# Layer 3's first values made in layer 2's last unit, in other tiles, and its position bias in tiles of two heads

## The chip, the cores and the metric

The kernel runs on one NeuronCore of a Trainium2 chip. The metric is the device time of one execution in microseconds (us). Five engines run side by side, each with its own queue of instructions: TensorE (PE, matrix products), VectorE (DVE), ScalarE (ACT), GpSimd (POOL) and SyncE (SP, which here only issues DMAs). Data lie in SBUF (128 partitions), and matrix products are written to PSUM, which this kernel uses as eight banks of 128 partitions by 512 numbers of float32.

## The reference

The input x has shape [8, 512, 128]. Four layers follow one another, each x = x + s * silu(ffn), where s is a token mixer and both are computed from the normalised x. Layers 0 and 1 are attentions with mixtures of experts. Layer 2 is a gated delta rule (a recurrence over chunks of the sequence) with a mixture of eight experts. Layer 3 is:

```python
def _L3_attn_ref(x, Wq, Wk, Wv, Wo, bo, rel_pos_bias):   # x: [8, 512, 128], 16 heads of 64
    q = (x @ Wq).reshape(B, T, H, dh).transpose(0, 2, 1, 3)
    k, v = ...                                             # the same with Wk, Wv
    logits = jnp.einsum('bhqd,bhkd->bhqk', q, k)
    logits = (logits + causal + bias) / dh                 # bias depends on i - j, clipped at 128
    probs = jax.nn.softmax(logits, axis=-1)
    out = jnp.einsum('bhqk,bhkd->bhqd', probs, v).transpose(0, 2, 1, 3).reshape(B, T, H * dh)
    return out @ Wo + bo

def _L3_ffn_ref(x, w_gate, w_up, w_down):                  # hidden size 384, weights dequantised
    return jnp.einsum('bsh,dh->bsd', silu(gate) * up, wd)
```

## The kernel before

**The order of the work.** PE's instructions run in the order in which the program writes them (`manual_schedule`); DVE, ACT, POOL and SP are put in order by a scheduler that works from its own estimates. Pieces of work are Python generators: `step(g, n)` issues the next n pieces of g, `drain(g)` all that are left. So where a piece is stepped decides where its matmuls stand in PE's queue.

**Tiles.** A pool hands out buffers by tag: a tag with one buffer (`bufs=1`, the default of pool `wf`) can be given to a second tile only when the first one's last reader is done, and what writes the second tile waits for that. Pool `wk` is opened and closed with each layer, so that layer 3's `wk` and `lp` tiles lie in memory that layer 2's pools give up at their end; pool `wf` ("wk23") lives through layers 2 and 3. `psS` is a pool of six PSUM banks with one tag, `psA` of two. `evac` (L73) copies a bank to SBUF, by turns with ACT (L77) and DVE (L79).

**Layer 2** has eight units u (half of the batches, a quarter of the sequence). In unit u's twelve half-rounds, `rounds` (L1074) steps by turns the scan (`delta_scan`, L1644: per chunk pk, rhs, pu, U, pn, stn, po), the experts, the inverse of unit u+1, the front of unit u+2, the output of unit u−1 (`delta_output`, L1684) and the combination of the experts (`combine2`, L1405: POOL gathers rows of the experts' results through indirect DMAs, L1341, two tiles g per unit of two buffers each, so the gathers of unit u wait for the reads of unit u−2; DVE L1434 to L1438 and ACT L1436 weigh them; POOL adds to x, L1441). In the last unit, u = 7, one piece of `weights3` (L1958) is stepped in each half-round: layer 3's weights are loaded into `wf` tiles that layer 2 no longer needs, those of the feed-forward net are dequantised and transposed (L1986), and batch 0 is normalised (`normed3`, L1781: DVE L109 to L118, then four transposes ptxnT and one copy to xnT). What is left of the generators is drained after unit 7, `weights3` last: the output of unit 7 (Vb scaled by POOL L1699, poT, pg, s), the combination, and the rest of `weights3`.

Of the tiles of layer 2 that matter here, `chan0` (the keys and queries by channel, [P, 2, 512] in all), `Kd` ([P, 512]) and `AO` ([P, 512]) lie in `wk` with three buffers each, `chan1` and the rest in `wf`.

**Layer 3** (`layer3`, L1731) first has the bias loaded: `position_bias` makes one tile of 16 heads x 512 per partition in `lp`, of which DVE clears the first 256 columns (four memsets, L1954) and SP loads the others (four DMAs). Then `inputs3(0)` (L1788) makes the values of batch 0: eight products pv of 128x512, for the four row tiles t and the two halves i of the heads (i = 0: heads 0 to 7), each copied by `evac` into a tile v3 of `wk`. After that comes one loop over half steps r; new, i = divmod(r, 2) is a group (b, g) of two heads of batch b and half i of its rows:

- `scores3` of the group: PE writes ps (one bank for i = 0, four for i = 1), DVE adds the bias and finds the greatest (L1833), ACT takes the exponentials (L1837), POOL scales by the sum (L1840).
- `summed3`, four half steps behind: av, the products of the probabilities and v. Group g uses heads 2g and 2g + 1, so groups 0 to 3 use v of i = 0 and groups 4 to 7 of i = 1.
- `transposed3`, three half steps behind: transposes ptp (L1850) in two banks or three, each copied to PT by `evac`.
- for i = 0, `project3` of the next group: pq and pk, each copied by `evac`; and, in every other group, a piece of `ffn3`: pg and pu, read by ACT L1904 and DVE L1905 and L1906.
- for i = 1, `projected3` of an earlier group, and two pieces of `inputs3(b + 1)`, which starts with group 0 of batch b and so has made the next batch's pv by b's group 5 or so.

All of ps, ptp, pq, pk, pg, pu, po, pv and ptxnT take their banks from `psS`; av and the sum of projections have one bank each in `psA`.

Of the kernel before, what the change touches and what calls it, by code (L numbers as in the profile page):

```python
# [9 lines left out]
F32 = mybir.dt.float32  # L10
I32 = mybir.dt.int32
AF = mybir.ActivationFunctionType
ALU = mybir.AluOpType
AX = mybir.AxisListType

B, S, D = 8, 512, 128
# [15 lines left out]
def tile_kernel(ctx: ExitStack, tc: tile.TileContext, w: dict, out: bass.AP):  # L32
# [1021 lines left out]
    def layer2():  # L1054
        nonlocal wk, fw, sm2
        with ExitStack() as lx:
            lp = lx.enter_context(tc.tile_pool(name="l2", bufs=1))
            fw = lx.enter_context(tc.tile_pool(name="fw2", bufs=3))
            wk = lx.enter_context(tc.tile_pool(name="wk2", bufs=1))
            sm2 = lx.enter_context(tc.tile_pool(name="sm2", bufs=4))  # L1060
            dram = lx.enter_context(tc.tile_pool(name="dram2", bufs=1, space=bass.MemoryType.DRAM))
            c = dict(lp=lp, dram=dram, units={}, xn_d=shared["xn_d"], rs2=shared["rs2"], lg=shared["lg"], ln=shared["ln"])
            c["eo_d"] = dram.tile([8 * CAP + 1, D], F32, name="l2eo_d")
            c["idx_d"] = dram.tile([P, CAP // 16], F32, name="l2idx_d")
            c["s_d"] = dram.tile([2 * NT, P, 4 * D], F32, name="l2s_d")
            with tc.manual_schedule(engines={mybir.EngineType.PE}):
                front = delta_front(0, c)
                step(front)
                loaded2(c)
                N = 2 * NT  # L1070
                out = iter(())
                weights = weights3()

                def rounds(u, experts, combined, n_experts):  # L1074
                    nonlocal out
                    scan = delta_scan(u, c)
                    inverse = delta_inverse(u + 1, c) if u + 1 < N else iter(())
                    front = delta_front(u + 2, c) if u + 2 < N else iter(())
                    for r in range(12):
                        step(scan)  # L1080
                        step(experts)
                        if not u and r > 1:
                            step(experts)
                        step(inverse)
                        if r > 1:
                            step(front)
                        if r % 3 < n_experts:
                            step(experts)
                        step(out)
                        if u > 3:  # L1090
                            step(combined)
                        if u == N - 1:
                            step(weights)
                    drain(scan, inverse, front, out)
                    out = delta_output(u, c)

                with tc.tile_pool(name="route2", bufs=1) as rp:
                    routed = route2(rp, c)
                    drain(front)
                    front = delta_front(1, c)  # L1100
                    for _ in delta_inverse(0, c):
                        step(front)
                    drain(front)
                    rounds(0, routed, iter(()), 0)
                    drain(routed)
                with tc.tile_pool(name="ex2", bufs=1) as ep:
                    experts = experts2(ep, c)
                    combined = combine2(ep, c)
                    for u in range(1, N):
                        rounds(u, experts, combined, 1)  # L1110
                    drain(out, experts, combined, weights)
# [338 lines left out]
    def delta_front(u, c):  # L1450
# [71 lines left out]
        for i, parts in enumerate((((0, None, G), (1, gam, V)), ((0, beta, G), (1, None, V)))):  # L1522
            byt = wf.tile([P, 2, 4, 4, 32], F32, tag="byt", name=f"byt{i}{nm}", bufs=1)
            for k, part in enumerate(parts):
                scaled(byt[:, k], *part)
            x = (wf if i else wk).tile([P, 2, 4, 4, 32], F32, tag=f"chan{i}", name=f"chan{i}{nm}", bufs=1 if i else 3)
            V.transpose(x.rearrange("p a c h i -> p (a c h i)"), byt.rearrange("p a c h k -> p (a c h k)"))
            chan.append(x)
        r["KT"], r["QgT"] = chan[0][:, 0], chan[0][:, 1]
        kd = r["Kd"] = wk.tile([P, 4, 4, 32], F32, tag="Kd", name=f"Kd{nm}", bufs=3)  # L1530
        scaled(kd, 0, wend, G)
        Vb = r["Vb"] = wk.tile([P, 4, 4, 64], F32, tag="Vb", name=f"Vb{nm}", bufs=4)
        G.tensor_tensor(Vb, y[:, :, 256:].rearrange("p c (h k) -> p c h k", k=64), bcast(hbeta.rearrange("p (c h) -> p c h", h=4), 3, 64), ALU.mult)
# [2 lines left out]
    def delta_inverse(u, c):  # L1536
# [21 lines left out]
        def level():  # L1558
            n = len(ao)
            if n < 5:  # L1560
                a = wk.tile([P, 16, 32], F32, tag="AO", name=f"AO{nm}_{n}", bufs=3)
                G.tensor_tensor(a, AT, bcast(c["lv"][:, n, :], 1, 16), ALU.mult)
                ao.append(a)

# [166 lines left out]
    def layer3():  # L1731
        nonlocal wk
        with ExitStack() as lx:
            lp = lx.enter_context(tc.tile_pool(name="l3", bufs=1))
            wk = lx.enter_context(tc.tile_pool(name="wk3", bufs=2))
            c = dict(lp=lp, v={}, qk={}, P={}, PT={}, th={}, s={}, **shared["w3"])
            c["bias"] = position_bias(lp, shared["bias"])
            bo = lp.tile([1, NT, D], F32, name="l3bo")
            for t in range(NT):
# [7 lines left out]
            n = 2 * len(groups)  # L1747

            with tc.manual_schedule(engines={mybir.EngineType.PE}):
                drain(inputs3(0, c))  # L1750
                for k in "qk":
                    project3(k, *groups[0], c)
                ffn, done, inputs = iter(()), iter(()), iter(())
                for r in range(n + 7):
                    new, i = divmod(r, 2)
                    if new < len(groups):
                        b, g = groups[new]
                        if g == 0 and i == 0:
                            inputs = inputs3(b + 1, c) if b + 1 < B else iter(())
                            ffn = ffn3(b, c)  # L1760
                        scores3(b, g, i, c)
                    for lag, stage in ((4, summed3), (3, transposed3)):
                        if 0 <= r - lag < n:
                            stage(*groups[(r - lag) // 2], (r - lag) % 2, c)
                    if i == 0:
                        for k in "qk" if new + 1 < len(groups) else "":
                            project3(k, *groups[new + 1], c)
                        if g % 2 == 0:
                            step(ffn)
                    at = r - 7  # L1770
                    if at >= 0 and i:
                        projected3(*groups[at // 2], c)
                        if groups[at // 2][1] == 7:
                            done = finish3(groups[at // 2][0], c)
                    if i:
                        step(inputs, 2)
                    else:
                        step(done)
                drain(ffn, done)
# [7 lines left out]

    def inputs3(b, c):  # L1788

        if b:  # L1790
            yield from normed3(b, c)
        v = c["v"][b] = wk.tile([P, NT, 1024], F32, tag="v3", name=f"v3_{b}")
        for t in range(NT):
            for i in range(2):
                pv = psS.tile([P, S], F32, tag="S", name=f"pv3_{b}_{t}_{i}")
                mm(pv, c["xnT"][b][:, t * P : (t + 1) * P], c["wv"][:, i * S : (i + 1) * S])
                evac(v[:, t, i * S : (i + 1) * S], pv)
                yield

    def project3(n, b, g, c):  # L1800
# [6 lines left out]
    def scores3(b, g, i, c):  # L1807
# [22 lines left out]
        parts = [(2 * n + j, c["P"][b, g, j][:, qb * N[qb] // 2 : qb * N[qb] // 2 + N[qb]], pss[j, qb], j, qb)  # L1830
                 for n, qb in enumerate(qbs) for j in range(2)]
        for n, p, src, j, qb in parts:
            V.tensor_tensor_reduce(p, src, c["bias"][:, 2 * g + j, (3 - qb) * P :], 1.0, NEG, ALU.add, ALU.max, mx[:, n : n + 1])  # L1833
            if n % 2:
                V.tensor_scalar(mx[:, n - 1 : n + 1], mx[:, n - 1 : n + 1], -1.0, None, ALU.mult)  # L1835
        for n, p, _, _, _ in parts:
# [31 lines left out]
    def summed3(b, g, i, c):  # L1868
# [3 lines left out]
        for kb in ((0,), (1, 3, 2))[i]:  # L1872
            k, at = PLACES[kb]
            for j in range(2):
                h = 2 * g + j
                mm(c["av"][64 * j : 64 * j + 64, kb * P :], c["v"][b][:, kb, 64 * h : 64 * h + 64],
                   c["PT"][b, g, j, k][:, at : at + S - kb * P], start=kb == 0, stop=kb == 2)
        if i:
            x = c["aT", b, g] = wk.tile([P, S], F32, tag="aT", name=f"aT3_{b}_{g}")
# [67 lines left out]
    def position_bias(pool, flat):  # L1947


        n = 3 * P  # L1950
        bias = pool.tile([P, H8, S], F32, name="l3bias")
        skewed = flat[:, 0 : P * (n - 1)].rearrange("h (p n) -> p h n", n=n - 1)
        for h in range(0, H8, 4):
            V.memset(bias[:, h : h + 4, 0 : 2 * P], 0.0)  # L1954
            nc.sync.dma_start(bias[:, h : h + 4, 2 * P :], skewed[:, h : h + 4, P - 1 : 3 * P - 1])
        return bias

    def weights3():  # L1958
# [21 lines left out]
        for raw, (n, key, _, tag) in zip(raws, names):  # L1980
# [6 lines left out]
            c[key] = wf.tile([P, NT, P], F32, tag=tag, name=f"l3{n}")[:, 0:3, :]  # L1987
            evac(c[key], pt[:, 0 : 3 * P].rearrange("p (c o) -> p c o", o=P))
            yield
        c["xnT"] = {}  # L1990
        yield from normed3(0, c)

    with tc.tile_pool(name="x12", bufs=1) as x12:
        with tc.tile_pool(name="fw", bufs=8) as fw:
# [27 lines left out]
```

## Time and profile before

| what | us |
| --- | --- |
| median of 3 runs | 3906.91 (3903.22 to 3912.37) |
| the profiled execution | 3900.36 |
| its span | 3898.6 |
| PE busy | 3563.5 (91%), 32622 matmuls |
| DVE, ACT, POOL busy | 2321.6, 1780.3, 1457.5 |
| granted clock of PE over the span | 0.952 |

The profile is one execution, taken by the hardware profiler. A timeline row reads: start, duration (of all that are merged in the row), engine, line, operation, written tile <- read tiles, shapes, count, and in brackets how long the engine was idle before it and what ended that. Times of a row count from the start of the span. A row of stretches gives its bounds, its length, busy time of PE, PEld (weight loads), DVE, ACT and POOL, the granted clock of PE as a share of its full speed, the DMA engines' busy share and GB/s. On the page's PE and PEclk rows each digit stands for a fortieth of the span, in tenths. Layer 2's scan of unit 7 ends near 3054, layer 3's first scores begin at 3095.32, and its steady part lasts to about 3889.

### The profile page before, as it was taken

What the parts mean: (1) busy time and instruction counts of PE and PEld (TensorE: products, weight loads), DVE (VectorE), ACT (ScalarE), POOL (GpSimd) and SP (SyncE); (2) the same over time, 40 slices, a digit from 0 to 9 for tenths busy, and PEclk for the clock granted to TensorE, in tenths of its full rate; (3) what the DMA queues carried; (4) which work ended last, traced back from release to release, by engine and by line L of the source; (5) the groups of instructions that cost most, each with busy time, mean ns of one, the idle gap of its engine ahead of it and who ended that gap; (6) DMA issues with size and microseconds to landing.
All of it is one profiled execution on the core that took longest, in us unless ns stands there. A gap on an engine that the chain in (4) does not pass through costs nothing.

```text
span 3898.6 us, 84883 instructions
## 1 busy us (share of the span) xinstructions
PE 3563.5 (91%) x32622; PEld 1701.0 (44%) x32622; DVE 2321.6 (60%) x7395; ACT 1780.3 (46%) x3916; POOL 1457.5 (37%) x2072
## 2 busy tenths in 40 slices
PE   5999999999999999999999986589886699999998
PEld 2444344444344333333333333456665455555555
DVE  5556656665656555556555664554555766666665
ACT  1355454455454545455555553122221355555554
POOL 1234334334443423333333333453464533333333
PEclk7999999999999999999999997799997899999999
DMA  4100101100011232322222222012112200000000
GB/s 114 46 10 31 31 11 30 30 19 26 27 40 49 78 94 76 84 74 70 69 72 72 71 76 68 5 30 52 32 41 63 48 1 4 4 4 4 4 4 6
DMA packets 139059, 162.93 MB, mean 42 GB/s; under 512 B 29835, under 2 KB 79666, under 8 KB 138528
## 3 DMA queue, kind: packets, MB, share of 16 engines
q1 hardware_dynamic: 135328, 150.69, 13.5%
q0 software_dynamic: 3328, 6.82, 1.0%
q8 instruction: 258, 4.23, 0.5%
q14 instruction: 145, 1.19, 0.1%
HBM read 129.84 MB, written 29.96 MB: 41 GB/s over the span
## 4 chain that ended last, share of the span: by engine, by line
PE 74%; DVE 13%; POOL 5%; issue 3%; ACT 3%; SPq 1%; DMA 1%; POOLq 0%; DVEq 0%; ACTq 0%
PE pt L82 12%; PE ph L82 12%; PE po L82 10%; PE av L82 10%; PE ps L82 8%; PE ptp L1850 3%; PE py L82 3%; PE pk L82 2%; PE s L82 2%; PE pq L82 2%; ACT P L1837 2%; PE pv L82 2%; DVE P L1833 1%; PE pY L82 1%; PE pth L552 1%
## 5 line engine op out<-in xcount | busy, mean ns | idle before, releaser
L522 DVE CUSTOM_DVE_ANT_0 l0junk<-ps,l0junk 128x512 f32<-128x512 f32 (+3 forms) x1024 | 502.1, 490 | 383.2 <-PE ps L82 311.9
L1012 POOL TENSOR_TENSOR h<-h,C 128x512 f32<-128x512 f32 x256 | 326.0, 1273 | 641.4 <-ACT h L1010 592.4
L578 ACT ACTIVATE PT<-pt 128x512 f32<-128x512 f32 (+1 forms) x768 | 360.7, 524 | 405.9 <-PE ps L82 365.4
L829 DVE TENSOR_REDUCE nm<-ps 128x1 f32<-128x512 f32 x512 | 331.6, 684 | 268.2 <-PE ps L82 267.3
L1840 POOL TENSOR_SCALAR P<-P,l 128x128 f32<-128x128 f32 (+3 forms) x512 | 262.7, 532 | 516.6 <-DVE l L1838 360.6
L82 PE MATMUL ps<-l0kA,l0qA 32*128 32x128 f32 (+3 forms) x2048 | 417.7, 486 | 16.7 <-DVE mx L522 11.3
L1837 ACT ACTIVATE P<-P,mx 128x128 f32<-128x128 f32 (+3 forms) x512 | 281.3, 550 | 300.3 <-DVE mx L1835 294.7
L582 POOL TENSOR_SCALAR_AFFINE_SELECT PT<-PT 128x256 f32<-128x256 f32 x512 | 202.0, 407 | 496.1 <-ACT PT L578 494.2
L82 PE MATMUL pt<-l0qA,l0kA 32*128 32x512 f32 (+3 forms) x2048 | 374.4, 470 | 2.1 <-DVE nm L829 1.2
L82 PE MATMUL ps<-l1kA,l1qA 32*128 32x512 f32 x1024 | 333.9, 651 | 33.0 <-DVE nm L829 31.9
L867 ACT ACTIVATE PT<-pt 128x512 f32<-128x512 f32 x512 | 275.9, 595 | 159.5 <-PE ps L82 130.2
L82 PE MATMUL av<-PT,vl0v 128*9 128x512 f32 (+3 forms) x3072 | 315.3, 498 | 1.2 <-POOL PT L582 1.2
L82 PE MATMUL ph<-xnT,l1e 128*128 128x512 f32 x512 | 292.3, 654 | 7.9 <-DVE H L856 3.2
L82 PE MATMUL pt<-l1qA,l1kA 32*128 32x512 f32 x1024 | 272.3, 645 | 0.3 <-ACT PT L867 0.3
L1010 ACT ACTIVATE h<-h 128x512 f32<-128x512 f32 x272 | 171.3, 630 | 217.1 <-DVE h L1007 194.0
L82 PE MATMUL po<-h,l1e 128*128 128x512 f32 x512 | 266.0, 601 | 0.0
L82 PEld LDWEIGHTS pt<-l0qA,l0kA 32*128 32x128 f32 x2048 | 165.6, 185 | 207.2 <-DVE mx L522 66.9
L1833 DVE CUSTOM_DVE_ANT_0 P<-ps,l3bias 128x128 f32<-128x128 f32 (+3 forms) x512 | 225.2, 486 | 39.5 <-PE ps L82 37.5
L671 POOL TENSOR_TENSOR h<-h,C 128x512 f32<-128x512 f32 x128 | 163.1, 1275 | 81.9 <-ACT h L669 63.5
L82 PEld LDWEIGHTS ps<-l0kA,l0qA 32*128 32x128 f32 x2048 | 164.7, 190 | 55.3 <-DVE mx L522 37.0
L669 ACT ACTIVATE h<-ph,l0b 128x512 f32<-128x512 f32 x192 | 131.9, 687 | 100.8 <-PE ph L82 98.4
L82 PE MATMUL av<-PT,v 128*64 128x128 f32 (+3 forms) x1024 | 173.1, 445 | 4.4 <-ACT PT L77 2.6
(523 smaller groups left out, 6368.6 us busy)
## 6 DMA issues: line engine op xcount, KB each, us to landing
C<-wd SPq DMA_DIRECT2D x288, 256.0 KB
qd<-qf SPq DMA_DIRECT2D x24, 256.0 KB
kd<-kf SPq DMA_DIRECT2D x24, 256.0 KB
l0qA<-qd SPq DMA_DIRECT2D x256, 16.0 KB
l0kA<-kd SPq DMA_DIRECT2D x256, 16.0 KB
l2e<-in_L_ffn_w_dram SPq DMA_DIRECT2D x16, 256.0 KB
l3flat<-l3short SPq DMA_DIRECT2D x16, 192.0 KB
l2eo_d<-eo SPq DMA_DIRECT2D x8, 320.0 KB
```

Of the source, the lines that this page charges most:

```text
L82: T.matmul(out_, lhsT, rhs, start=start, stop=stop)
L522: V.tensor_tensor_reduce(c["junk"][:, : (qb + 1) * P], pss[j][:, at], c["mask"][:, (3 - qb) * P :], 1.0, NEG, ALU.add, ALU.max, mx[i][:, q ...
L578: A.activation(p[:, j % 2, :N], pss[j][:, :N], AF.Exp)
L582: G.affine_select(out=own, in_=own, compare_op=ALU.is_ge, fill=0.0, base=0, pattern=[[0, 2], [1, P]], channel_multiplier=-1)
L671: G.tensor_tensor(h, h, C[b, e], ALU.mult)
L829: V.tensor_reduce(nm[g][:, j, qb : qb + 1], pss[j], AX.X, ALU.max, negate=True)
L867: A.activation(Pt[j // 2][:, j % 2, :], pss[j], AF.Exp)
L1010: A.activation(h, h, AF.Square)
L1012: G.tensor_tensor(h, h, C[b, u - u % 2][:, u % 2, :], ALU.mult)
L1833: V.tensor_tensor_reduce(p, src, c["bias"][:, 2 * g + j, (3 - qb) * P :], 1.0, NEG, ALU.add, ALU.max, mx[:, n : n + 1])
L1837: A.activation(p, p, AF.Exp, bias=mx[:, n : n + 1], accum_out=l[:, n : n + 1])
L1840: G.tensor_scalar(p, p, l[:, n : n + 1], 1.0, ALU.mult, ALU.mult)
```

## The change

Three things:

1. In unit 7 two pieces of `weights3` are stepped per half-round instead of one, and `weights3` ends with `inputs3(0)`, not just `normed3(0)`: the eight pv of batch 0 are issued there, and `layer3` no longer does it.
2. `chan0`, `Kd` and `AO` move to `wf`; `chan0` and `Kd` get three tags of one buffer instead of one tag of three. The values of even batches are put into tiles with the tags chan00 and chan02 (asked for once per i, [P, 2, 512] each, of which the half i is used), Kd0, Kd2, and two of AO's buffers; the values of odd batches into a single tile v3 (`bufs=1`; it had two buffers).
3. The bias lies in eight tiles of two heads, l3bias0 in the tag chan01 of `wf` and the seven others in `lp`, with eight memsets and eight DMAs.

```diff
@@ rounds (layer 2)
                         if u == N - 1:
-                            step(weights)
+                            step(weights, 2)
@@ delta_front, delta_inverse
-            x = (wf if i else wk).tile([P, 2, 4, 4, 32], F32, tag=f"chan{i}", name=f"chan{i}{nm}", bufs=1 if i else 3)
+            x = wf.tile([P, 2, 4, 4, 32], F32, tag="chan1" if i else f"chan0{u % 3}", name=f"chan{i}{nm}")
...
-        kd = r["Kd"] = wk.tile([P, 4, 4, 32], F32, tag="Kd", name=f"Kd{nm}", bufs=3)
+        kd = r["Kd"] = wf.tile([P, 4, 4, 32], F32, tag=f"Kd{u % 3}", name=f"Kd{nm}")
...
-                a = wk.tile([P, 16, 32], F32, tag="AO", name=f"AO{nm}_{n}", bufs=3)
+                a = wf.tile([P, 16, 32], F32, tag="AO", name=f"AO{nm}_{n}", bufs=3)
@@ layer3
-                drain(inputs3(0, c))
                 for k in "qk":
                     project3(k, *groups[0], c)
@@ inputs3
-        if b:
-            yield from normed3(b, c)
-        v = c["v"][b] = wk.tile([P, NT, 1024], F32, tag="v3", name=f"v3_{b}")
+        yield from normed3(b, c)
+
+        if b % 2:
+            v = wk.tile([P, NT, 2, S], F32, tag="v3", name=f"v3_{b}", bufs=1)
+            v = [v[:, t, i, :] for t in range(NT) for i in range(2)]
+        else:
+            v = [wf.tile([P, 2, S], F32, tag=f"chan0{u}", name=f"v3_{b}_c{u}")[:, i, :] for u in (0, 2) for i in range(2)] + [wf.tile([P, S], F32, tag=f"Kd{u}", name=f"v3_{b}_k{u}") for u in (0, 2)] + [wf.tile([P, S], F32, tag="AO", name=f"v3_{b}_a{i}", bufs=3) for i in range(2)]
+        c["v"][b] = v
         for t in range(NT):
             for i in range(2):
...
-                evac(v[:, t, i * S : (i + 1) * S], pv)
+                evac(v[2 * t + i], pv)
@@ position_bias
-        bias = pool.tile([P, H8, S], F32, name="l3bias")
+        bias = [pool.tile([P, 2, S], F32, name=f"l3bias{g}") if g else wf.tile([P, 2, S], F32, tag="chan01", name="l3bias0")
+                for g in range(H8 // 2)]
...
-        for h in range(0, H8, 4):
-            V.memset(bias[:, h : h + 4, 0 : 2 * P], 0.0)
-            nc.sync.dma_start(bias[:, h : h + 4, 2 * P :], skewed[:, h : h + 4, P - 1 : 3 * P - 1])
+        for g, x in enumerate(bias):
+            V.memset(x[:, :, 0 : 2 * P], 0.0)
+            nc.sync.dma_start(x[:, :, 2 * P :], skewed[:, 2 * g : 2 * g + 2, P - 1 : 3 * P - 1])
@@ weights3
-        c["xnT"] = {}
-        yield from normed3(0, c)
+        c["xnT"], c["v"] = {}, {}
+        yield from inputs3(0, c)
```

The indexing of v and of the bias in `summed3` and `scores3` follows the new tiles; the products and their order are the same.

More of the change, by code (lines that the diff above doesn't have):

```diff
@@ L1735, in layer3 @@
             wk = lx.enter_context(tc.tile_pool(name="wk3", bufs=2))
-            c = dict(lp=lp, v={}, qk={}, P={}, PT={}, th={}, s={}, **shared["w3"])
+            c = dict(lp=lp, qk={}, P={}, PT={}, th={}, s={}, **shared["w3"])
             c["bias"] = position_bias(lp, shared["bias"])
@@ L1832, in scores3 @@
         for n, p, src, j, qb in parts:
-            V.tensor_tensor_reduce(p, src, c["bias"][:, 2 * g + j, (3 - qb) * P :], 1.0, NEG, ALU.add, ALU.max, mx[:, n : n + 1])
+            V.tensor_tensor_reduce(p, src, c["bias"][g][:, j, (3 - qb) * P :], 1.0, NEG, ALU.add, ALU.max, mx[:, n : n + 1])
             if n % 2:
@@ L1875, in summed3 @@
                 h = 2 * g + j
-                mm(c["av"][64 * j : 64 * j + 64, kb * P :], c["v"][b][:, kb, 64 * h : 64 * h + 64],
+                mm(c["av"][64 * j : 64 * j + 64, kb * P :], c["v"][b][2 * kb + h // 8][:, 64 * (h % 8) : 64 * (h % 8) + 64],
                    c["PT"][b, g, j, k][:, at : at + S - kb * P], start=kb == 0, stop=kb == 2)
```

## The prediction

> **What bounds the kernel now.** I read four views. First the page: its share of busy time by slice, and its chain.
>
> ```profile
> PE   5999999999999999999999986589886699999998
> PEclk7999999999999999999999997799997899999999
> ```
>
> ```profile
> PE 74%; DVE 13%; POOL 5%; issue 3%; ACT 3%; SPq 1%; DMA 1%; POOLq 0%; DVEq 0%; ACTq 0%
> ```
>
> PE carries the end nearly everywhere. It falls off only in the stretch of slices 24 to 32, layer 2 (a slice is 97.5 us); the change touches that layer's last unit and the hand-over to layer 3 (3028 to 3096, slice 32). Then the stretches: columns are busy time of PE, PEld, DVE, ACT and POOL, granted clock, DMA share, GB/s.
>
> ```profile
> 3054.00:3069.20 15.20, 0.08 (x2) 0.01 (x1) 9.28 (x57) 1.52 (x3) 12.50 (x15) 0.57 0.51 65
> 3096.50:3889.00 792.50, 783.89 (x4416) 436.21 (x4416) 519.95 (x1829) 452.77 (x1350) 272.65 (x520) 1.00 0.01 3
> ```
>
> In layer 3 PE is busy 783.89 of 792.50 us: any new wait of PE there is paid in full, once for each of the 64 groups (a batch's two heads) that it touches. Third, PE's and POOL's timelines over the hand-over:
>
> ```profile
> 3055.94 0.94 POOL L1341 DMA_INDIRECT g<-l2eo_d,l2row  x1 [0.30 <-issue]
> ...
> 3067.23 1.91 POOL L1699 TENSOR_TENSOR Vb<-Vb,on 128x1024 f32<-128x1024 f32 x1
> ```
>
> ```profile
> 3069.19 1.12 PE L1713 MATMUL poT<-ident,Vb 128*128 128x128 f32 x4 [15.12 <-POOL Vb L1699]
> ...
> 3088.09 3.78 PE L82 MATMUL pv<-l3wvq,xnT 128*128 128x512 f32 x4 [5.46 <-ACT v L77]
> ...
> 3095.32 1.14 PE L82 MATMUL ps<-kT,qT 64*128 64x128 f32 x8 [0.72 <-ACT kT L77]
> ```
>
> PE idles 15.12 us until POOL has issued the last gathers of the experts' rows and scaled Vb. Then layer 2's last output, its combine (DVE, then POOL's x, ending at 3087.42), and only then layer 3's first copy of v, since its tiles lie in memory that layer 2 gives up last. Last, a group of layer 3 (batch 2, group 4), PE and ACT:
>
> ```profile
> 3336.42 1.14 PE L82 MATMUL ps<-kT,qT 64*128 64x128 f32 x8
> 3337.49 1.08 PE L82 MATMUL av<-PT,v 128*64 128x512 f32 x4
> 3338.50 1.53 PE L1850 MATMUL ptp<-ident,P 128*128 128x128 f32 x12
> 3339.86 1.02 PE L82 MATMUL pq<-xnT,l3wvq 128*128 128x512 f32 x2
> 3340.73 1.02 PE L82 MATMUL pk<-xnT,l3wk 128*128 128x512 f32 x2
> ```
>
> ```profile
> 3339.23 0.40 ACT L1837 ACTIVATE P<-P,mx 128x128 f32<-128x128 f32 x1 [2.98 <-DVE mx L1835]
> ...
> 3341.21 1.04 ACT L77 COPY PT<-ptp 128x512 f32<-128x512 f32 x2
> ```
>
> PE never waits here, though ACT empties ptp only after the four exponentials: six PSUM banks (pool psS) let PE write pk before that copy.
>
> **Part 1: eight pv into unit 7.** Removed after layer 2's end: 16 pv matmuls and their copies. Before, they filled 3077.22 to 3091.66, but beside the combine, so the path loses only what lies behind POOL's last x at 3087.42: the v copies of ACT (1.56) and PE's last four (3.78). DVE's four l3bias memsets end at 3091.83 (1.07 apart) and stand ahead of DVE's v copies and of qT (3094.08). In the changed order seven memsets of 512 elements stand there. Bounds for one: 0.53 (half of 1.07) and 1.07; I take 0.62, as half the work and the 0.16 gap stay. That is 4.3 in place of 4.3, and the copies of 2.42 go; but fourteen small operations of batch 1's normalisation (0.11 each, as pairs of 0.22 to 0.24) move ahead of the first scores. Gain here 0.8 (2.42 less 14 times 0.11, and less 0.06 of memsets).
>
> Added in unit 7: in PE's written order ptxnT and the pv now stand among the scan's matmuls, and whatever they wait for holds back the scan behind them. ptxnT needs the four gl of DVE (2.70 us in this trace, ending 3049.15, between POOL's x and gathers); the scan's pu behind it ran at 3045.74, and goes to about 3049.6. The first pv wait for the copy of ptxnT, the matmuls take 0.9 each at the full clock and up to 1.8 at half, and four v copies on DVE (0.69 each, after the 0.66 of DVE's copies in layer 3) stand ahead of the g operation of L1437, which ends at 3054.82 and which POOL's gathers at 3055.94 wait for, because it frees their tile. Walking this chain: pu's 3.9 and two pv behind it (0.9 to 1.0 each) put the last chunk's pk from 3049.54 to about 3055.3; from there to L1437's end it is 5.3 as before (3049.54 to 3054.82, DVE full, the v copies in the place of PE's waits), so 3060.6 to 3060.7. The gathers begin near 3060.9 instead of 3055.94: +5.0 for them, Vb, poT and the combine behind. A gl that leaves the combine's chain gives back 0.4, projections q and k between the output's matmuls cost 0.5. Sum: +5.0 + 0.5 − 0.4 − 0.8 = **+4.3**. Bounds: −1 if POOL's slack of 1.1 (3054.82 to 3055.94) and idle PE take it all; +9 if the pv run at the half clock (eight more times 0.5 to 0.9).
>
> **Part 2: where v lies.** Even batches ask for the tiles chan00 and chan02 of [P,2,S] twice each, once for each i, and use one half. Each tag has one buffer. So the second (i = 1, heads 8 to 15) cannot be written until every av of the first (heads 0 to 7, groups 0 to 3) has run. In the built order ACT's copy of pv_0_0_1 indeed stands among the exponentials of group 5, likewise for batches 2, 4, 6. Until then two pv sit in PSUM: **two of psS's six banks are held** (a pv of 512 columns fills one), for batch 0 from unit 7 to group 4, for batches 2, 4, 6 from group 2 or 3 of the batch before to group 4: 34 of 64 groups run on four banks.
>
> What that costs I get by giving each layer 3 tile the bank that the built kernel gives it, with its start and its release from this trace, and delaying PE where the bank is still full. The group above as a sample: pk must now wait for the first PT copy. Two take 1.04 from 3341.21, the second starting 0.46 to 0.58 after the first; the first ends at 3341.78, so pk starts 1.05 late (plus 0.06, the usual pause between a copy's end and PE). Then the last ps (3344.57) waits for h L1906, at 3344.75: 0.18 to 0.24. The group pays 1.35. Over the layer: batches 2 and 4 pay 5.4 and 5.7, batch 6 4.3, batches 1, 3, 5 1.2 each (their later half), batch 0 5.1 from group 2 on: 24.2 with the pause, 21.5 without. I take **+21.5**. Bounds: 14, if the delayed PE lets ACT and DVE catch up (ACT is 57% busy, DVE 65%), 26 with the pause and its repeats. Groups 0 and 1 of batch 0, where the pipeline fills: **+2.5** (0 to 3.5).
>
> **Part 3: the clock.** PE pauses of 1.1 to 1.7 us (1.2 to 2.5 in a group) now come in about ten groups, and smaller ones in a dozen more. Rows of this trace: between 3011.85 and 3025.50 the clock was 0.50, though PE was busy 8.32 of 13.65 us and no pause among these matmuls was above 2.33. In all stretches of 3.41 us at the full clock, the next was at half in 30 of 31 where PE was busy under half, 10 of 19 between 0.5 and 0.6, 4 of 14 to 0.7, 2 of 35 to 0.8. A pause of 1.1 leaves 0.68, one of 1.7 leaves 0.5. Some five drops, each 1.7 to 2.5 us (half of what PE does in such a stretch at half clock): **+5**, from 0 to 18 (one drop in each of the eight to ten heaviest groups).
>
> The Trainium skill, "TensorE: Matmul & The Clock Gate", section "Why this matters for your kernels", asks only for no idle gap above about 3 us. By it this term would be nothing and the sum 28; the stretch at 3011.85 speaks against it.
>
> **Part 4: the bias in tiles of two heads.** Eight DMAs for four; seven go at layer 2's release as the four did, and the first group needs only heads 0 and 1, loaded early. L1833's instructions keep number, size and order. Nothing, covered by ps 8 us behind the release; if the cover went, a DMA's delay of some 2 us (sr<-l2s_d, 2.58 on the chain), inside the range.
>
> **Sum:** 4.3 + 21.5 + 2.5 + 5 = +33.3 on the profiled 3900.36 (span 3898.6): 3933.7. That run lies 6.55 under the median of the three shown (3906.91; 3903.22 to 3912.37), so 3940.
>
> **Rivals.**
> (a) *Four banks are enough*: the copies keep ahead, PE's wait shrinks to nothing, and only the hand-over counts: 3906.91 + 4.3 = 3911, or 3906 with −1, not slower by a measurable amount. For it: ACT and DVE are idle over a third of the layer. Against: the idle time lies before the exponentials (2.98), not after. It decides where PT's first copy ends before pk's start: it would have to come 1.05 earlier.
> (b) *The change does what it says*, v is out of PSUM at once, and L1437 isn't delayed. The 7.87 between layer 2's release (3087.45) and the first ps (3095.32) shed 0.8 if the memsets stay as in part 1, up to 7 if nothing of layer 3's start is behind them: 3900 to 3906. Against: the double request of one buffer, and ACT's built order.
> (c) *The clock drops in most groups that pause*: 18 in place of 5, 3953.
> (d) *Unit 7's pv run at half clock* and gathers start 9 later: 3945.
>
> **How the numbers follow.** My forecast (3926 to 3948) 0.58; (c) 0.15; (d) 0.12; a smaller bank cost, 14 or less with no clock drop (3915 to 3926), 0.07; (a) 0.05; (b) 0.03. Leaving out (a), (b) and the far end of (c): 3916 to 3957. A measurement of this kernel tells 0.2%, 7.8 us, from no change. Faster beyond it: (b) with a little more than I worked out, 0.02. Within it (to 3914.7): (a) and the rest of (b), with a corner of the small bank cost, 0.08. Slower: the others, 0.90.
>
> **What would show it.** In the changed profile's PE timeline: pk and ps in groups 2 to 4 of even batches with idle before them released by ACT PT L77, ACT kT or DVE h; v<-pv copies of ACT long after their pv; half-clock slices in layer 3; DVE L1437 and the gather that was at 3055.94 about 5 us later; POOL's last x near 3092. Part 1 is wrong if the gathers start before 3057; part 2 if PE's busy time in layer 3 stays 99%, or if ACT copies pv_0_0_1 before group 3. What would make the whole wrong is PE waiting elsewhere: a kernel that is faster says that the banks were free.

## The result

The changed kernel takes 3938.43 us (median of four runs, 3937.14 to 3942.33) against 3907.17 for the kernel before: 1.0081 times its time, 95% interval 1.0068 to 1.0094, so 31 us slower (27 to 37). The profiled execution took 3942.33, with a span of 3940.4.

The page's rows by slice and its chain look almost as before; a loss of under one per cent does not show there:

```profile
PE   5999999999999999999999985688986699999998
PEclk8999999999999999999999997789987899999999
...
PE 72%; DVE 14%; ACT 5%; POOL 4%; issue 4%; SPq 1%; DMA 0%; POOLq 0%; DVEq 0%; ACTq 0%
```

ACT's share of the chain has grown from 3% to 5%, PE's has shrunk from 74% to 72%: work that used to lie beside PE now lies between two of its matmuls. The stretches say where (busy time of PE, PEld, DVE, ACT, POOL; granted clock of PE; DMA share; GB/s). The first row is the start of layer 3 from its first ps, the second the rest of it:

```profile
3110.71:3115.40 4.69, 4.69 (x11) 2.10 (x12) 4.69 (x37) 0.47 (x3) 0.00 (x0) 0.50 0.53 178
3115.40:3940.00 824.60, 795.65 (x4414) 438.58 (x4412) 517.32 (x1806) 455.02 (x1351) 272.76 (x520) 0.99 0.01 4
```

PE's matmuls are the same in number (4424 from the first ps to the end), but the layer is longer: from the first ps to the end of the span it takes 829.7 where it took 803.3. The group that the prediction took as its sample (batch 2, group 4), on PE and on ACT:

```profile
3363.36 1.14 PE L82 MATMUL ps<-kT,qT 64*128 64x128 f32 x8
3364.43 1.08 PE L82 MATMUL av<-PT,v_c 128*64 128x512 f32 x4
3365.44 1.53 PE L1854 MATMUL ptp<-ident,P 128*128 128x128 f32 x12
3366.80 1.02 PE L82 MATMUL pq<-xnT,l3wvq 128*128 128x512 f32 x2
3368.77 1.13 PE L82 MATMUL pk<-xnT,l3wk 128*128 128x512 f32 x2 [0.94 <-ACT PT L77]
3369.73 1.02 PE L82 MATMUL pg<-xnT,l3gate 128*128 128x512 f32 x2
3370.59 1.02 PE L82 MATMUL pu<-xnT,l3up 128*128 128x512 f32 x2
3371.54 2.11 PE L82 MATMUL ps<-kT,qT 64*128 64x512 f32 x8
```

```profile
3366.17 0.40 ACT L1841 ACTIVATE P<-P,mx 128x128 f32<-128x128 f32 x1 [2.98 <-DVE mx L1839]
...
3368.15 1.04 ACT L77 COPY PT<-ptp 128x512 f32<-128x512 f32 x2
```

Before, pk followed pq by 0.87; now by 1.97, with ACT's copy of PT named as what ended the wait: 1.10 more, where the prediction had 1.05 and a pause of 0.06. ACT's idle time ahead of its exponentials is the same 2.98 in both. The last row of PE shows a second loss that no bracket names. The same eight ps in the kernel before:

```profile
3343.39 1.56 PE L82 MATMUL ps<-kT,qT 64*128 64x512 f32 x8
```

They took 1.56 and take 2.11, because the timeline merges matmuls of one kind and a wait for DVE's h inside the row counts as the row's time. So PE's busy time in layer 3 has grown from 785.07 to 800.34 with the same matmuls, and the list of its waits there (us in all, times, longest) adds up to less than the 26 us that the layer lost:

```profile
PE pk L82 <- ACT PT L77: 12.0, 12, 1.6
PE av L82 <- ACT PT L77: 2.4, 10, 0.8
PE ps L82 <- DVE mx L1837: 0.5, 2, 0.4
```

In the kernel before, the wait of pk was not in that list at all; its longest entries were

```profile
PE av L82 <- ACT PT L77: 2.6, 10, 0.8
PE ptp L1850 <- POOL P L1840: 1.5, 1, 1.5
```

The hand-over, on POOL and PE:

```profile
3073.99 1.28 POOL L1341 DMA_INDIRECT g<-l2eo_d,l2row  x1 [4.01 <-DVE g L1437]
...
3085.59 1.91 POOL L1699 TENSOR_TENSOR Vb<-Vb,on 128x1024 f32<-128x1024 f32 x1
```

```profile
3061.14 0.84 PE L125 MATMUL ptxnT<-ident,gl 128*128 128x128 f32 x3 [0.92 <-DVE gl L118]
3061.91 0.65 PE L82 MATMUL pu<-rhs,TT 32*32 32x64 f32 x32
3062.71 1.99 PE L82 MATMUL pv<-l3wvq,xnT 128*128 128x512 f32 x4
...
3087.55 1.12 PE L1713 MATMUL poT<-ident,Vb 128*128 128x128 f32 x4 [12.22 <-POOL Vb L1699]
...
3110.71 2.08 PE L82 MATMUL ps<-kT,qT 64*128 64x128 f32 x8 [15.77 <-issue]
```

The first ps needs the copy of q, which on DVE stands behind the seven memsets of the bias:

```profile
3106.33 3.73 DVE L1959 MEMSET l3bias<- 128x512 f32 x7 [0.66 <-POOL x L1441]
3109.98 0.63 DVE L79 COPY qT<-pq 128x512 f32<-128x512 f32 x1
```

Starts from the beginning of the span can't be compared here: 8.2 us of the changed execution's lateness arose before layer 2, in instructions that the change doesn't touch, and 5.7 in layer 2, which the last experiment takes up. So the table counts from a fixed place, the last matmul pU of unit 7's inverse (3028.57 before, 3042.45 after).

| | before | after | difference |
| --- | --- | --- | --- |
| first gather that waits for L1437 | 27.38 | 31.54 | +4.2 |
| POOL's last x (end of the combine) | 58.86 | 63.71 | +4.9 |
| first ps of layer 3 | 66.75 | 68.26 | +1.5 |
| layer 3, first ps to the end | 803.31 | 829.72 | +26.4 |

The two stages together give 27.9; the remaining 3.4 of the difference of the medians lie within their interval.

### The profile page after: what moved, and what is told of

It reads as the page before. It is cut to its first block, busy times and chain, and to the rows that moved or that the text cites. A ratio compares the mean times of both kernels' runs of the same rounds, so it can differ in the third digit from the quotient of the medians.

```text
span 3940.4 us, 84869 instructions
## 1 busy us (share of the span) xinstructions
PE 3587.3 (91%) x32622; PEld 1709.0 (43%) x32622; DVE 2322.9 (59%) x7399; ACT 1782.7 (45%) x3916; POOL 1457.8 (37%) x2072
## 4 chain that ended last, share of the span: by engine, by line
PE 72%; DVE 14%; ACT 5%; POOL 4%; issue 4%; SPq 1%; DMA 0%; POOLq 0%; DVEq 0%; ACTq 0%
PE pt L82 12%; PE ph L82 12%; PE po L82 10%; PE av L82 9%; PE ps L82 8%; ACT P L1841 3%; PE py L82 3%; PE ptp L1854 2%; PE s L82 2%; DVE P L1837 2%; PE pk L82 2%; PE pv L82 2%; PE pq L82 1%; PE pth L552 1%; PE pmx L503 1%
## 5 line engine op out<-in xcount | busy, mean ns | idle before, releaser
L82 PE MATMUL ps<-kT,qT 64*128 64x128 f32 (+3 forms) x1024 | 187.2, 460 | 17.6 <-issue 15.8
```

The source lines that it names most:

```text
L82: T.matmul(out_, lhsT, rhs, start=start, stop=stop)
```

## The experiments

Each set of runs went to one chip, but not all sets to the same one. On the chip of the first set (e1_once, e2_one_held, e7_three_held, e4_twice_alone) the kernel before takes 3981.61. It was not traced there, but in the traces of this set layer 2 is some 60 us longer than elsewhere. So ratios to the kernel before on the same chip are compared, and lengths of stages. Layer 3 of the kernel before and of the changed one differed by at most 0.14 between their traces (last experiment); that it has the same length on the first set's chip is assumed.

**One request per tile.** The theory (A): two PSUM banks are held by pv that cannot be copied until the tile's first half is read. The edit asks once and uses both halves:

```diff
-            v = [wf.tile([P, 2, S], F32, tag=f"chan0{u}", name=f"v3_{b}_c{u}")[:, i, :] for u in (0, 2) for i in range(2)] + ...
+            v = [x[:, i, :] for x in [wf.tile([P, 2, S], F32, tag=f"chan0{u}", name=f"v3_{b}_c{u}") for u in (0, 2)] for i in range(2)] + ...
```

> The changed kernel, but chan00 and chan02 are asked for once per batch and both halves of the heads lie in that tile, so no pv is held in PSUM. Theory A (held banks): layer 3, from its first ps to the end of the span, takes 829.7 in the changed kernel and 803.3 in the kernel before; it goes back to 803 to 804, PE's waits for PT disappear from pk, and the time falls by about 26 to 3908 to 3916. Rival B (the hand-over and the tiles moved in layer 2 carry the loss): the time stays at 3930 or above, and what stands ahead of the first ps (3110.71 against 3095.32) stays late by more than 10.

Measured: 1.0006 times the kernel before (0.9997 to 1.0015), layer 3 804.78. PE's waits in layer 3 are back to

```profile
PE av L82 <- ACT PT L77: 2.5, 10, 0.8
PE ptp L1854 <- POOL P L1844: 1.5, 1, 1.5
PE av L82 <- ACT aT L77: 0.8, 4, 0.2
```

The wait of pk is gone, and with it 24.9 of layer 3's 829.7; rival B falls. Layer 3 stays 0.8 above the 803 to 804 expected; where that comes from is shown further down.

**The dose.** One bank held instead of two, and three:

```diff
 # e2_one_held: chan00 asked for twice, chan02 once
+ [wf.tile([P, 2, S], F32, tag="chan00", ...)[:, i, :] for i in range(2)] + [x[:, i, :] for x in [wf.tile([P, 2, S], F32, tag="chan02", ...)] for i in range(2)]
 # e7_three_held: as the changed kernel, and
- [wf.tile([P, S], F32, tag=f"Kd{u}", name=f"v3_{b}_k{u}") for u in (0, 2)]
+ [wf.tile([P, S], F32, tag="Kd0", name=f"v3_{b}_k{u}") for u in (0, 2)]
```

> The changed kernel, but only chan00 is asked for twice: one bank of six is held. Theory A: the walk over the kernel before's own times, with the banks that this kernel gets, says 4.7 (no pause) to 5.5 of waits from group 2 on, against 21.5 to 24.2 with two banks, and a little in the first two groups: layer 3 takes 808 to 811, the time is 3913 to 3922. Rival B: as the changed kernel, 3935 to 3940, since its hand-over is the same.

> The changed kernel, but Kd0 is asked for twice too (in place of Kd0 and Kd2), so that three banks are held from group 2 of a batch on and three are left. Theory A: the same walk gives 72.6 to 77.5 of waits from group 2 on, and some 6 to 10 in the first two groups: layer 3 takes 880 to 895, the time is 3985 to 4005. If PE's clock falls in such groups, as the prediction had it for two banks (5 us, up to 18), half-clock stretches appear in layer 3 and the time passes 4010. Rival B: 3940 to 3950.

Measured: 1.0017 (1.0006 to 1.0029) and 1.0206 (1.0190 to 1.0222), that is 7 and 82 over the kernel before on this chip, where the expectations, written for the other, amount to 6 to 15 and 78 to 98. By layer 3:

| banks held | layer 3 | over e1_once | the walk on the times of before, from group 2 on |
| --- | --- | --- | --- |
| 0 (e1_once) | 804.78 | 0 | 0 |
| 1 (e2_one_held) | 810.60 | 5.8 | 4.7 to 5.5 |
| 2 (the changed kernel) | 829.72 | 24.9 | 21.5 to 24.2 |
| 3 (e7_three_held) | 881.76 | 77.0 | 72.6 to 77.5 |

The cost grows far faster than the number of banks, and the walk follows it. The measured differences contain the first two groups of batch 0, for which the prediction adds 2.5 with two banks and the expectation 6 to 10 with three: the sums are 24.0 to 26.7 against 24.9, and 78.6 to 87.5 against 77.0. The prediction's clock term can be read from the same run: e7_three_held's PE waits, the only stretch of layer 3 after its start at half clock, and the stretch before that one:

```profile
PE pq L82 <- ACT PT L77: 21.5, 12, 2.1
PE pk L82 <- ACT PT L77: 15.2, 19, 0.9
PE ps L82 <- DVE mx L1837: 5.1, 15, 0.4
```

```profile
3432.00:3435.40 3.40, 3.40 (x6) 1.32 (x5) 0.69 (x1) 0.61 (x2) 0.65 (x2) 0.50 0.02 5
3428.50:3431.90 3.40, 1.54 (x8) 0.83 (x7) 1.05 (x4) 2.82 (x10) 1.09 (x3) 1.00 0.00 0
```

The recorded clock changes in steps of 3.41 us. In ten such steps of this run's layer 3 PE was busy between 0.46 and 0.57 of the time; the clock fell after one of them, the least busy, with a pause of 1.85. With two banks held it never fell once layer 3 was under way.

**The double request alone**, in the kernel before:

```diff
-        v = c["v"][b] = wk.tile([P, NT, 1024], F32, tag="v3", name=f"v3_{b}")
+        if b % 2: ...    # one tile, bufs=1
+        else:
+            v = [wk.tile([P, 2, S], F32, tag=f"vc{u}", name=f"v3_{b}_c{u}", bufs=1)[:, i, :] for u in (0, 2) for i in range(2)]
+            rest = wk.tile([P, 4, S], F32, tag="vr", name=f"v3_{b}_r", bufs=1)
+            v = v + [rest[:, n, :] for n in range(4)]
```

> The kernel before, changed in one thing: the values of even batches lie in tiles of layer 3's own pool, of which the two for the first two row tiles have one buffer each and are asked for twice. Values stay where they were made, layer 2 and the bias are untouched. Theory A: this alone costs 22 to 30 (21.5 to 24.2 from group 2 on, the rest where the pipeline fills): 3929 to 3937, with layer 3 at 826 to 832. Rival B: no change, 3903 to 3911.

Measured: 1.0067 (1.0052 to 1.0082), which is 27 of 3981.61; layer 3 828.81. The double request is enough for the loss, without any of the rest.

**The parts of the hand-over.** First the moved tiles and the bias alone (`step(weights)` as before, and `drain(inputs3(0, c))` in `layer3` again); then the pv right behind the scan of unit 7; then, in addition, the memsets on POOL:

```diff
 # e3_tiles_only, against e1_once
-                            step(weights, 2)
+                            step(weights)
...
+                drain(inputs3(0, c))
 # e5_behind_scan, against e1_once
-                            step(weights, 2)
+                            step(weights)
...
-                    drain(out, experts, combined, weights)
+                    step(out)
+                    drain(weights, out, experts, combined)
 # e6_pool_memset, against e5_behind_scan
-            V.memset(x[:, :, 0 : 2 * P], 0.0)
+            G.memset(x[:, :, 0 : 2 * P], 0.0)
```

> The changed kernel with chan00 and chan02 asked for once, and batch 0's values made where they were before the change, after layer 2's end: only the moved tiles and the bias in tiles of two heads are left of it. If moving chan0, Kd and AO to the other pool costs nothing in layer 2 (theory A: the 5.7 by which layer 2's part ahead of unit 7's scan is longer in the changed profile is scatter of one execution), the ratio is 0.9993 to 1.0007, with layer 3 at 803 to 805. Rival C (the moved tiles make layer 2 longer by 3 to 6): 1.0008 to 1.0015. Against e1_once the hand-over, from the last po of unit 7 on, tells what the pv in unit 7 cost: 1 to 2 for e1_once by theory A.

> As e1_once, but the rest of layer 3's preparation with the eight pv is drained right behind the scan of unit 7 and ahead of its output, so that the pv stand where PE idles (15.12 us in the kernel before, waiting for POOL's Vb) and hold back neither the scan nor the g operation of L1437. Theory A: the gathers start as early as before, and from layer 2's release to the first ps it takes 4.5 as in the changed kernel in place of 7.87: faster than before by 3 to 4.5, ratio 0.9988 to 0.9993. Rival B (a gain made in the hand-over is given back by the combine, which is bound by DMA and POOL alone): ratio 0.9997 to 1.0005.

> As e5_behind_scan, with the bias's memsets on POOL, which has nothing else to do at layer 2's release, in place of DVE, whose seven memsets (3.73 in the changed profile) stand ahead of the copy of q that the first ps waits for. Theory A: another 3 to 3.5 faster: 6 to 8 under the kernel before, ratio 0.9980 to 0.9986. Rival B: the first scores then wait for something else (a bias DMA behind the memset, or kT), and it is as e5_behind_scan.

| | ratio (95%) | last pU to POOL's last x | from there to the first ps | layer 3 |
| --- | --- | --- | --- | --- |
| before | 1 | 58.86 | 7.90 | 803.31 |
| changed | 1.0081 (1.0068 to 1.0094) | 63.71 | 4.55 | 829.72 |
| e3_tiles_only | 1.0002 (0.9992 to 1.0012) | 59.17 | 4.54 | 805.01 |
| e5_behind_scan | 0.9999 (0.9991 to 1.0008) | 59.32 | 4.55 | 805.47 |
| e6_pool_memset | 0.9988 (0.9979 to 0.9998) | 59.13 | 0.82 | 805.07 |

Three things follow. The 3.35 between POOL's last x and the first ps are gained by the moved tiles and the bias in eight tiles, without the pv in unit 7 (e3_tiles_only): DVE's four copies of v (2.42) no longer come behind the memsets, since they don't go to memory that layer 2 holds until then, and seven small memsets take 3.73 where four large ones took 4.13. Making the pv inside unit 7's scan adds nothing to that and costs 4.5 on the way there (63.71 against 59.17); behind the scan it costs nothing. And the memsets on DVE are nearly all that is left of the wait: on POOL, behind its last x, they take 3.40, and the wait falls from 4.55 to 0.82.

```profile
3100.46 3.40 POOL L1960 MEMSET l3bias<- 128x512 f32 x7
```

Some expectations missed here. That pv in unit 7 cost 1 to 2 was too little. e5_behind_scan was to be 3 to 4.5 faster: from the last pU to the first ps it is 2.9 shorter (63.86 against 66.75), but its layer 3 is some 2 longer than 803.3, which takes back most of that, as in e3_tiles_only. Its ratio so lies where rival B had it, but not for rival B's reason. e6_pool_memset, at 0.9988, is a little above the 0.9980 to 0.9986 expected, by the same 2 us.

**Where those 2 us go.** In the changed kernel, in e3_tiles_only and in e6_pool_memset PE runs at half clock when layer 3 begins, after having been idle for 15.77, 6.54 and 12.05. The rows of e6_pool_memset:

```profile
3101.23 2.08 PE L82 MATMUL ps<-kT,qT 64*128 64x128 f32 x8 [12.05 <-ACT kT L77]
3103.24 2.07 PE L82 MATMUL pq<-xnT,l3wvq 128*128 128x512 f32 x2
3105.10 1.43 PE L82 MATMUL pk<-xnT,l3wk 128*128 128x512 f32 x2
```

These rows took 1.14, 1.12 and 1.02 in the kernel before, where the last pv and q and k ran directly ahead of the first ps. The test keeps PE of e6_pool_memset busy there with work that is not part of the reference:

```diff
+                warm = psA.tile([P, S], F32, tag="A", name="warm", bufs=1)
+                for j in range(28):
+                    T.transpose(warm[:, j % 4 * P : (j % 4 + 1) * P], xs[4 + j // 7][:, 2, :], ident)
```

> As e6_pool_memset, with 28 transposes of 128x128 on PE behind the first projections q and k, of the four x tiles that the combine of unit 6 has just added to, into a bank that nobody reads. They do no work of the reference; they only keep PE busy in the last 5 to 6 us ahead of the first ps. Theory A: layer 3 takes 804.8 to 805.5 in the kernels without held banks, not 803.3 as in the kernel before, because PE idles some 12 us before the first ps and runs its first 4.7 us at half clock; with the transposes the clock is full at the first ps, layer 3 takes 803.2 to 803.6, and the kernel is 1.5 to 2 faster than e6_pool_memset (6 to 7.5 under the kernel before, ratio 0.9981 to 0.9985). Rival B: the 1.5 to 2 come from the values' new places or the bias tiles, and layer 3 stays at 805; or the transposes end after the copy of k and delay the first ps by 1 or more.

```profile
3094.25 5.47 PE L1755 MATMUL warm<-ident,x 128*128 128x128 f32 x28 [5.74 <-POOL x L1442]
3100.59 1.14 PE L82 MATMUL ps<-kT,qT 64*128 64x128 f32 x8 [0.86 <-ACT kT L77]
3101.65 1.13 PE L82 MATMUL pq<-xnT,l3wvq 128*128 128x512 f32 x2
3102.62 1.02 PE L82 MATMUL pk<-xnT,l3wk 128*128 128x512 f32 x2
```

The first rows are back at their old durations and layer 3 takes 803.68, so the half clock accounts for 1.4 of the 1.8 by which e6_pool_memset exceeds 803.3; 0.4 stay unexplained. The time is 0.9985 (0.9976 to 0.9994) of the kernel before, the lowest ratio of all versions. That e9_warm is faster than e6_pool_memset is shown by the stage (1.4), not by the two ratios, whose intervals overlap.

**Is layer 2 slower with the moved tiles?** Up to the last pU it took 586.27 in the trace of the kernel before and 591.97 in that of the changed one. So each was traced twice more, in turn, on one chip, with nothing changed:

> The kernel before, unchanged, for a second trace of it. From layer 2's first pY to its last pU the one trace of it took 586.27, and five traces of kernels with chan0, Kd and AO in the other pool 588.6 to 596.6 on chips of the same speed. Theory A (scatter): this one lies anywhere between 585 and 596. Rival C (the moved tiles cost 3 to 6): 585 to 588, and below both traces of the changed kernel on the same chip.

> The changed kernel, unchanged, for a second trace. From the last pU to the first ps: 68 to 69 (68.26 in the first trace), layer 3 829.5 to 830. Layer 2 up to the last pU: theory A 586 to 597, rival C above both traces of the kernel before on the same chip, by 3 to 6.

> The kernel before a third time. Layer 2 up to the last pU: theory A 585 to 596, in no order with the changed kernel's; rival C 585 to 588. From the last pU to the first ps 66 to 67.5, layer 3 803 to 803.6 by both.

> The changed kernel a third time: layer 3 829.5 to 830 by both; layer 2 up to the last pU by theory A in no order with the kernel before's, by rival C 3 to 6 above them.

| | layer 2 to the last pU | from there to the first ps | layer 3 |
| --- | --- | --- | --- |
| before, three traces | 586.27, 588.04, 586.70 | 66.75, 65.30, 66.28 | 803.31, 803.38, 803.37 |
| changed, three traces | 591.97, 589.24, 583.90 | 68.26, 67.62, 66.85 | 829.72, 829.83, 829.69 |

The changed kernel's 583.90 is the lowest of all six, so these traces don't bear rival C out. They don't settle it either: the single traces of e3_tiles_only, e5_behind_scan, e6_pool_memset and e9_warm, which have the moved tiles too, lie at 588.6 to 596.6, above all three of the kernel before, though on another chip than two of those three. The timed ratios of those four runs, less their differences in the hand-over and in layer 3, leave −0.4 to 1.5 us for all that lies ahead, each to within about 4. A cost of a few microseconds can't be excluded. The hand-over is 1.5 longer on average (67.6 against 66.1; the changed kernel's second, 67.62, lies a little under the 68 to 69 expected), and layer 3 repeats to 0.15: that is where 26.3 to 26.5 of the loss lie, in every trace.

## Why the prediction was right

The predicted 3940 was met (3938.43), and so was the cause; but of its four terms only the largest was well sized.

- **What bounds the kernel.** That a new wait of PE in layer 3 would be paid in full held: e1_once and the changed kernel differ by 24.9 there, and nothing of it is given back later.
- **Part 2, the held banks: right in place and size.** 21.5 from group 2 on and 2.5 for the first two groups, 24.0 in all; measured 24.9. The sample group showed its 1.10 in the row that was named. The lower bound (14, if ACT and DVE caught up) did not come into play. The likely reason, argued from the sample and not tested: PT's copy comes behind the exponentials of the same group's scores, so that a later PE makes the copy later too.
- **Part 1, the hand-over: right in mechanism, too dear.** Predicted +4.3, measured +1.5. The gathers, +4.2, were near the 5.0 that was worked out, and the combine's end (+4.9) as well. The term that was mis-sized is "Gain here 0.8": it is 3.35. Seven memsets took 3.73, 0.53 each, the lower bound and not the 0.62 taken; and the fourteen small operations of batch 1 stand behind the copy of q, not ahead of it. Rival (d) is out: the pv in unit 7 ran at full clock (four in 1.99).
- **Part 3, the clock: wrong in place and size.** Predicted 5 (0 to 18) for drops caused by the new pauses. With two banks held (pauses of up to 1.6) there was none in layer 3, and with three (up to 2.1) one. The prediction applied to layer 3 a table of steps of 3.41 us that came almost wholly from the three layers before it. Of the steps with PE busy between 0.5 and 0.6, the clock fell there after 5 of 8 in layers 0 and 1 (for instance at 2015.16, behind a pause of 1.65) and after 4 of 11 in layer 2, 9 of 19 in all where the prediction counted 10. In layer 3 of the changed kernel and of e7_three_held it fell after none of eight such steps. Those of the earlier layers that ended in a drop contain matmuls of 32 rows (32*32 and 32*128 in a timeline), those of layer 3 only matmuls of 64 and 128 rows; whether that makes the difference no run separates. What the clock did cost is 1.4 to 2 at the start of layer 3, after a gap of 6.5 to 16 us, and the prediction did not see that the pv it was glad to remove had brought the clock up (the last four ran at half clock, 3.78 in all, the first ps behind them at full). The Trainium skill ("TensorE: Matmul & The Clock Gate", "Why this matters for your kernels") asks for no idle gap above about 3 us between bursts of matmuls: for layer 3 that would have been the better guide, since it gives nothing for the pauses and a drop for the gap. But it is not a full rule here: the clock also fell behind pauses of 1.85 (e7_three_held) and of 1.65 (layer 1 of the kernel before), and the stretch of layer 2 shown in the prediction does not follow it.
- **Part 4, the bias:** nothing to be seen; e3_tiles_only, which has it, is as fast as the kernel before.

The sum, 33.3, was therefore nearer to the measured 31.3 than its terms deserve: by stages it should have been 24.9 + 1.5 (the start at half clock) + 1.5 (the hand-over) = 27.9, the lower part of the measured interval. Rival (a) is refuted by e1_once and the dose, rival (c) by the clock of the changed kernel itself, which stays full from 3115.40 to its last matmul. Rival (b) had two parts, v out of PSUM at once and L1437 not delayed. e1_once has the first alone and is no faster than before: the 3.35 gained behind POOL's last x are less than the 4.9 lost ahead of it, and the start at half clock costs 1.5 more. A gain comes only with the pv behind the scan and POOL's memsets.

## What to carry to other kernels

Before results are moved into tiles that have become free, go through each tag: how many buffers it has, how often it is asked for, and when the last reader of each tile is done. A second request of a tag with one buffer is no error and shows in no stage of its own; it holds whatever the copy would have emptied, here two of six PSUM banks, and the price can be walked on the old trace: start of each tile against the release of the one that had its bank. Where work is moved into an idle time, ask also which queue it is put in front of (the pv in the scan held back a gather some 10 us further on), and what its going leaves idle: PE, idle for 6.5 to 16 us ahead of layer 3 (e3_tiles_only, e6_pool_memset, the changed kernel), started that layer at half clock.

## What was not expected of the hardware

In layer 3 PE's clock stayed full through pauses that left it busy only 0.46 to 0.57 of ten stretches of 3.41 us (e7_three_held), falling after one, while in layer 2 a stretch of 13.65 us lay at half clock with 8.32 busy and no pause above 2.33, and in layer 1 one pause of 1.65 was enough for a drop (PE busy 1.77 of 3.42 us). POOL cleared 512 columns of float32 on 128 partitions no slower than DVE: seven memsets in 3.40 (e6_pool_memset) against 3.73 on DVE (the changed kernel). And with 28 transposes, 5.47 us of PE work that nobody reads, a stage that follows begins at full clock and is 1.4 shorter.
